# One more product by a 20-multiplication scheme, sums straight out of PSUM, and Strassen products for the two plain matrix products

## The chip, the cores and the metric

The kernel runs on one core of a Trainium2 chip. A core has a matrix engine (TensorE, PE in the profile; PEld is its loading of the stationary operand), a vector engine (VectorE, DVE), a scalar engine (ScalarE, ACT), GpSimd (POOL) and SyncE (SP), which here only issues transfers. Each works through its own instructions in order; they wait for each other by semaphores. Matrix results land in PSUM, eight banks of 512 float32 columns, here used as four pairs named b1, b3, b2_0 and b2_1. The metric is the device time of one execution in microseconds (us).

## What is computed

```python
out_lin = x @ lin_w.T + lin_b
xv = jnp.einsum('bf,efm->bem', x, weight)
zp = jnp.einsum('bf,efm->bem', jnp.square(x), jnp.square(weight))
interaction = 0.5 * jnp.sum(jnp.square(xv) - zp, axis=1)
return out_lin + interaction
```

x is 1024 x 512 (batch b, features f), weight is 64 x 512 x 512 (e, f, m), lin_w is 512 x 512, all float32. The large part is xv: a 1024 x 512 matrix times a 512 x 32768 one. Since zp is only summed over e, it needs the sum of the squared weights over e and then one 1024 x 512 by 512 x 512 product, like the linear part.

## The kernel before

The 512 columns m are taken in 22 groups: two of 16 columns, then twenty of 24 (`groups`, L133). A group has 64 times as many columns of the wide matrix, 1024 or 1536.

**Outer scheme.** Each group is one matrix product cut into 2 x 2 blocks and computed with seven block products instead of eight (Strassen in Winograd's form), taken in `ORDER` = 1, 6, 5, 2, 7, 4, 3. The operands from x, X1 to X7, are made once. The sums on the weight side (T1, T2, w12, w21) are made by transfers that add (`outer_sum`), and so are two of the sums of results (`outer_out`). The results go through the SBUF tiles oa, ob, oc and od: each product writes a `TARGET`, most add an `ADDEND` from an earlier product. A finished result is squared on ACT (`square`, L438), summed over e on DVE (`reduce`, L447) and put in `acc`. The weights' own squares and sums (`w_squares`) go to `w2_sum`.

**Inner schemes.** A block product is computed in one of two ways. `tree` (L630) is one more Strassen level: 7 products, each of two matmuls, of 384 columns in a wide group and 256 in a group of 16. `wide_tree` (L719) is a scheme for 4 x 2 blocks times 2 x 3 blocks with 20 products in place of 24, each one matmul of 256 columns; it is used for the outer products in `HK`, in wide groups only. It needs more operands of X, made by `widen` (L542) when the first wide group comes. Each matmul in float32 is two passes on PE. Both schemes start with sums of weights on POOL into tile t, keep partial sums in PSUM banks, copy some from bank to bank on ACT (L431, negated L430) so that products can go on adding to both copies, and let results leave PSUM by adds on DVE (`tt`, L413 to L421, `leave`). A tree uses b1, b3 and one of the b2 pairs; a wide tree uses one of b1 and b3 and both b2 pairs.

**How an addend comes in.** A result that leaves PSUM can have two addends: a partial sum of the same product, which is held in a tile p5 or p53 after a copy by ACT, and the outer addend. Normally DVE adds the first to the bank's content, and POOL adds the second in SBUF. For a product in `EARLY`, DVE instead adds the outer addend to a partial sum when that stands in the bank (`ahead`, or `leave` before the last product), and later adds the bank to the result, so there is neither the copy nor the add on POOL.

**Order.** The program is written as a list of operations with estimated costs (`Plan.add`). `Plan.order` plays them through like a queue on each engine, takes for PE the one with the smallest key among those that are ready, for the others the one whose latest time comes first, and so fixes each engine's order of instructions in advance. `AHEAD_OF` is a table of shifts, one for each operation, that moves latest times; SP's operations stand for the issue of transfers.

**Ends.** At the start x and lin_w are loaded, and the linear part runs as plain matmuls of 512 columns (L503): 8 row blocks x 4 parts of f. It is stored in DRAM with the bias. At the end -0.5 x squared is made on DVE (L916), `acc` and the linear part are read back and added (L930), and 32 matmuls of 512 columns (L950) multiply the squares with `w2_sum`; DVE adds both and the result is stored.

Of the kernel before, what the change touches and what calls it, by code (L numbers as in the profile page):

```python
# [12 lines left out]
AF = mybir.ActivationFunctionType  # L13
# [6 lines left out]
HK = (1, 5, 7)  # L20
EARLY = (2,)
# [14 lines left out]
SPARE = -99.0  # L36
AHEAD_OF = """
0:l 1:hvhc 2:3bp 3:hvw0 4:37v 5:338 6:3g7 7:34e 8:1o 9:33e a:33f b:-d c:369 d:-2 e:28 f:1 g:-1v h:-k i:-2k
j:-o k:-5 l:-26 m:8 n:7 o:i p:2a q:d r:15 s:b t:29 u:q v:-5 w:4 x:-k z:m 10:-9 11:d 12:-5 13:g 14:w 15:-2
16:10 17:-b 18:-e 19:17 1a:f 1b:1b 1c:l 1d:-14 1e:-c 1f:-3 1g:-11 1h:m 1i:7 1j:2 1k:8 1l:6 1m:-g 1n:-2 1o:-r  # L40
1p:-h 1q:m 1r:-r 1s:a 1t:5 1u:j 1v:-f 1w:3 1x:a 1y:o 1z:-g 20:3 21:-p 22:-g 23:g 24:2tw 25:2xs 26:f 28:38f
29:314 2a:-8 2b:-26 2c:9 2d:-4 2e:-8 2f:i 2g:-l 2h:-2 2i:d 2j:z 2k:-a 2l:13 2m:l 2n:m 2o:-7d 2p:-7 2q:-1 2r:1h
2s:-h 2t:-u 2u:ao 2v:-d 2w:-c 2x:-k 2y:7 2z:d 30:13 31:s 32:1u 33:-m 34:-j 35:-14 36:-i 37:-c 38:4 39:c 3a:18
3b:b 3c:-5 3d:l 3e:8 3f:1 3g:23u 3h:k 3i:1m 3j:g 3k:d 3l:1w1 3m:f 3n:-18 3o:-c 3p:5 3q:-i 3r:-g 3s:o 3t:-2
3u:-17 3v:3 3w:-q 3x:-t 3y:m 3z:m 40:-4 41:1rk 42:-a 43:-f 44:2 45:5 46:-1b 47:-1r 48:-4j 49:-s 4a:-t 4b:-3
4c:-o 4d:1d 4e:b 4f:2 4g:-r 4h:j 4i:-i 4j:1s 4k:-4 4l:4 4m:f 4n:3 4o:-7 4p:-l 4q:1j 4r:-b 4s:a 4t:c 4u:-2 4v:2
4w:m 4x:-1a 4y:-1 4z:-5 50:2 51:-2 52:-5 53:-5 54:r 55:x 56:13 57:n 58:20 59:1vi 5a:f 5b:-2 5c:1q 5d:-d 5e:1u1
5f:8 5g:-f 5h:3 5i:-2 5j:7 5k:36 5l:17 5m:-h 5n:-7 5o:10 5p:15 5q:i 5r:-w 5s:g 5t:f 5u:c 5v:-s 5w:1 5x:j 5y:6
5z:4d 60:e 61:13 62:d 63:-p 64:k 65:-b 66:17 67:-g 68:-k 69:-m 6a:1g 6b:x 6c:a 6d:-5 6e:5 6f:-7 6g:1e 6h:-4
6i:z 6j:-h 6k:-3h 6l:-22 6m:n 6n:-1n 6o:r 6p:y 6q:a 6r:10 6t:m 6u:-9 6v:-2 6w:2n 6x:-18 6y:-1h 6z:1 70:m  # L50
71:-1e 72:-k 73:-4 74:-3 75:-d 76:9 78:-o 79:-3 7a:-t 7b:-k 7c:-7 7d:-s 7e:b 7f:-9 7g:-1i 7h:-13 7i:19 7j:j
7k:1h 7l:-24 7m:c 7n:-2 7o:5 7p:-3 7q:q 7r:r 7s:q 7t:b 7u:1a 7v:v 7w:q 7x:-4 7y:-1p 7z:10 80:19 81:-o 82:m
83:c 84:-u 85:1 86:-1 87:-2 88:-4 89:-4 8a:-5 8b:-11 8c:3 8d:c 8e:-r 8f:x 8g:-w 8h:-u 8i:-5 8j:-1p 8k:-3
8l:-1e 8m:y 8n:o 8o:1f 8p:-1 8q:5 8r:-2 8s:1xv 8t:j 8u:7 8v:-7 8w:-f 8x:-u 8y:f 8z:1 90:e 91:6 92:-h 93:18
94:r 95:n 97:-1a 98:-c 99:-p 9a:-e 9b:8 9d:-11 9e:-3 9f:e 9g:-n 9h:-a 9j:-16 9k:-f 9l:-2 9m:h 9n:3 9o:f 9p:-5
9q:-2b 9r:v 9s:-18 9t:o 9u:o 9v:232 9w:8 9x:c 9y:-n 9z:d a0:-7 a1:-a a2:5 a3:-h a4:u a5:i a6:-d2 a7:8 a8:-n
a9:8 aa:-do ab:1a ac:i ad:-12 ae:11 af:2 ag:s ah:-n ai:-9 aj:-9 ak:3 al:l am:-fj an:-5 ao:2sx ap:d aq:13 ar:-4
as:2 at:t au:-9 av:-y aw:-l ax:-2 ay:9 az:v b0:-3 b1:-8 b2:l b3:-13 b4:g b5:-b b6:-1g b7:7 b8:-15 b9:-1 ba:-f
bc:-o bd:-b be:j bf:e bg:s bh:-1i bi:-1q bj:-1g bk:n bl:g bm:4 bn:a bo:-g bp:g bq:1 br:8 bs:-c bt:-1r bu:1e
bv:-1p bw:z bx:d by:m bz:-1f c0:-p c1:-5 c2:2 c3:q c4:-1j c5:-8 c6:j c7:e c8:-f c9:-b ca:5 cb:f cc:-k cd:1c  # L60
ce:-1n cf:-3 cg:-5 ch:-s ci:-m cj:-9 ck:-k cl:-7 cm:r cn:-a co:a cp:-n cq:-q cr:-10 cs:-w ct:b cu:-a cv:-10
cw:1g cx:-12 cy:j cz:-v d0:-14 d1:1b d2:-g d3:-g d4:8 d5:8 d6:-16 d7:n d8:j d9:-r da:-4 db:-13 dc:1d dd:-15
de:-9 df:16 dg:19 dh:d di:a dj:z dk:-a dl:-9 dm:-1w dn:-w do:-4 dp:p dq:b dr:-1w ds:2x dt:-b du:-e dv:-4 dw:3
dx:-t dy:g dz:8 e0:d e1:-5 e2:-g e3:-u e4:w e5:-r e6:j e7:4 e8:o e9:e ea:9 eb:a ec:-f ed:-16 ee:-l ef:k eg:-d
eh:-1g ei:i ej:-4 ek:-o el:-u em:5 en:-1f eo:-4 ep:5 er:7 es:s et:-1p eu:-9 ev:-b ew:o ex:i ey:-j ez:c f0:-14
f1:-u f2:-11 f3:5 f4:-l f5:c f6:-q f7:5 f8:k f9:-1 fa:-1e fb:1 fc:-1f fe:-j ff:-1 fg:5 fh:t fi:-q fj:-g fk:-8
fl:4 fm:-1o fn:10 fo:b fp:-3 fq:-13 fr:r fs:2 ft:-19 fu:1b fv:-t fw:-5 fx:-14 fy:-5 fz:-k g0:-6 g1:-6 g2:-2
g3:-1w g4:1o g6:-e g7:a g8:q g9:-d ga:-5 gb:8 gc:-h gd:9 ge:-5 gf:-7 gg:a gh:6 gi:-h gj:2 gk:-11 gl:-6 gm:4
gn:e go:1v gp:-14 gq:s gr:6 gs:-v gt:3 gu:3 gv:d gw:-6 gx:1q gy:-2 gz:-19 h0:-1m h1:-1h h2:-h h3:-5 h4:-g
h5:-14 h6:-2 h7:z h8:-j h9:f ha:-b hb:-6 hc:10 hd:-14 he:9 hf:e hg:-6 hh:-n hi:-a hj:y hk:-2 hl:-8 hn:6 ho:-t  # L70
hp:-g hq:-2 hr:-14 hs:c ht:4 hu:1 hv:a hw:-15 hx:-l hy:i hz:-d i0:-8 i1:-8 i2:-8 i3:11 i4:-7 i5:-13 i6:1h i7:b
i8:2 i9:7 ia:-8 ib:a ic:6 id:-m ie:2 if:4 ig:6 ih:-o ii:-a ij:-8 ik:n il:c im:u in:x io:-6 ip:a iq:-g ir:s
is:g it:l iu:-m iv:-1l iw:-2 ix:16 iy:-1o iz:-q j0:-y j1:-a j2:u j3:q j4:z j5:-1t j6:3 j8:-h j9:-c ja:12
# [947 lines left out]
```

## Time and profile before

| | |
|---|---|
| median of 3 runs | 1416.3 us (1412.21 to 1417.54) |
| profiled execution, own time | 1415.96 us |
| its span, first to last instruction | 1414.2 us |
| TensorE clock granted, mean | 0.997 |
| DMA | 251.76 MB, mean 178 GB/s |

The profile shows one execution. Lines name engine, source line (L464 is the matmul of the products), operation, written tile <- read tiles and form, the number of instructions after an x, then busy time and the mean of one in ns, then the idle time of the engine before them and what ended it. In the table by stretches each engine has its busy us and number of instructions, and the last three columns are the granted clock, the busy share of the transfer engines and GB/s. In the chain each row has start, length and what was worked on or waited for.

### The profile page before, as it was taken

The page shows a single profiled execution, that of the slowest core. Times are in us where ns is not written, and L with a number is a line of the kernel's source. Part 1 is how long each engine was busy: PE and PEld are TensorE (multiplying, and loading weights), DVE is VectorE, ACT ScalarE, POOL GpSimd, SP SyncE. Part 2 cuts the span into 40 slices and gives each one's busy share as a digit, 9 for nine tenths or more (in the row PEclk, how much of TensorE's full clock was granted, in tenths as well). Part 3 has the DMA queues.
Part 4 walks back from the last instruction along what each step waited for, and adds up shares of the span by engine and source line. Part 5 has one row for each costly group of instructions (what it writes and reads, how often), then busy time and mean ns, then how long its engine had stood idle before and what let it go on. Part 6 is the DMA issues. An engine that isn't in the chain of part 4 may idle for free.

```text
span 1414.2 us, 16647 instructions
## 1 busy us (share of the span) xinstructions
PE 1396.6 (99%) x5160; PEld 971.5 (69%) x5160; DVE 1100.0 (78%) x1461; ACT 806.0 (57%) x1293; POOL 1173.7 (83%) x1117
## 2 busy tenths in 40 slices
PE   8999989999999999999999999999999999999998
PEld 3887757767776766767676676777677677767663
DVE  2678678878878786887879688787968878796895
ACT  1456465656757465665656566565746556574642
POOL 5999978897979798797979879897987989788870
PEclk9999999999999999999999999999999999999999
DMA  8589596777949676795968678596958859694773
GB/s 260 164 192 227 135 202 153 165 188 161 228 120 228 160 178 171 167 223 117 230 159 192 160 180 208 131 222 146 216 143 195 197 132 221 135 238 109 163 193 112
DMA packets 92599, 251.76 MB, mean 178 GB/s; under 512 B 29472, under 2 KB 30496, under 8 KB 92512
## 3 DMA queue, kind: packets, MB, share of 16 engines
q0 software_dynamic: 26448, 134.49, 49.6%
q1 hardware_dynamic: 65488, 115.17, 24.0%
q8 instruction: 42, 0.69, 0.2%
q10 hardware_dynamic: 576, 1.05, 0.2%
q14 instruction: 45, 0.37, 0.1%
HBM read 127.04 MB, written 6.19 MB: 94 GB/s over the span
## 4 chain that ended last, share of the span: by engine, by line
PE 90%; POOL 4%; DMA 4%; DVE 1%; issue 1%; ACT 0%; SPq 0%; POOLq 0%; DVEq 0%; ACTq 0%
PE b L464 51%; PE b_r L464 18%; PE b_l L464 17%; POOL t L421 2%; PE b_r L950 1%; PE b_l L950 1%; DMA oc<-od 1%; DMA T<-T1a 1%; DMA oa<-xT 1%; PE b_l L503 1%; PE b_r L503 1%; DMA w<-weight 1%; POOL X L421 1%; DMA X<-xT 0%; POOL ob L456 0%
## 5 line engine op out<-in xcount | busy, mean ns | idle before, releaser
L464 PE MATMUL b<-t,X 128*128 128x384 f32 (+1 forms) x1504 | 518.5, 474 | 1.9 <-DVE ob L421 1.1
L464 PEld LDWEIGHTS b<-t,X 128*128 128x128 f32 x1504 | 276.1, 190 | 168.4 <-DVE oa L421 18.8
L421 POOL TENSOR_TENSOR t<-t,w 128x256 f32<-128x256 f32 (+1 forms) x200 | 232.6, 1287 | 9.0 <-PE b L464 5.7
L421 POOL TENSOR_TENSOR t<-w 128x768 f32<-128x768 f32 (+1 forms) x88 | 163.0, 1860 | 88.1 <-PE b_l L464 70.5
L438 ACT ACTIVATE oa<-oa 128x768 f32<-128x768 f32 (+1 forms) x176 | 142.8, 822 | 134.5 <-DVE oa L421 132.4
L464 PE MATMUL b<-w,X 128*128 128x384 f32 (+1 forms) x576 | 193.9, 469 | 0.1
L464 PE MATMUL b_l<-t,X 128*128 128x256 f32 x720 | 189.6, 381 | 3.9 <-ACT b_l L431 3.9
L464 PE MATMUL b_r<-t,X 128*128 128x256 f32 x600 | 167.9, 383 | 0.4 <-DVE ob L421 0.3
L447 DVE TENSOR_REDUCE acc<-oa 128x12 f32<-128x768 f32 (+1 forms) x176 | 161.6, 920 | 3.7 <-ACT oa L438 3.7
L447 DVE TENSOR_REDUCE w_sum<-wsq 128x12 f32<-128x768 f32 (+1 forms) x176 | 161.5, 920 | 1.1 <-ACT wsq L438 1.0
L464 PEld LDWEIGHTS b_l<-t,X 128*128 128x128 f32 x720 | 137.2, 191 | 32.2 <-ACT b_l L431 4.5
L464 PEld LDWEIGHTS b<-w,X 128*128 128x128 f32 x576 | 109.1, 190 | 56.5 <-ACT p L431 2.1
L464 PEld LDWEIGHTS b_r<-t,X 128*128 128x128 f32 x600 | 113.9, 191 | 47.7 <-issue 5.0
L438 ACT ACTIVATE wsq<-w 128x768 f32<-128x768 f32 (+1 forms) x132 | 107.3, 821 | 38.8 <-DVE w_sum L447 16.9
L421 DVE TENSOR_TENSOR oa<-b,oa 128x768 f32<-128x768 f32 (+1 forms) x88 | 82.0, 932 | 59.6 <-PE b L464 55.7
L421 POOL TENSOR_TENSOR t<-w,t 128x384 f32<-128x384 f32 (+1 forms) x96 | 107.7, 1122 | 2.4
L431 ACT COPY b<-b 128x768 f32<-128x768 f32 (+1 forms) x94 | 71.2, 757 | 60.3 <-PE b L464 58.0
L464 PE MATMUL b_r<-w,X 128*128 128x256 f32 x400 | 99.8, 380 | 0.0
L464 PE MATMUL b<-T,X 128*128 128x384 f32 (+1 forms) x264 | 91.3, 477 | 0.6 <-DMA T<-T1a 0.6
L421 DVE TENSOR_TENSOR oa<-b,oc 128x768 f32<-128x768 f32 (+1 forms) x66 | 61.2, 930 | 34.7 <-PE b L464 32.9
L464 PEld LDWEIGHTS b_r<-w,X 128*128 128x128 f32 x400 | 76.3, 191 | 14.3
L421 POOL TENSOR_TENSOR oc<-ob,p 128x512 f32<-128x512 f32 (+1 forms) x80 | 82.3, 1105 | 3.6 <-ACT p L431 2.0
(143 smaller groups left out, 2618.1 us busy)
## 6 DMA issues: line engine op xcount, KB each, us to landing
w<-weight SPq DMA_DIRECT2D x120, 384.0 KB, 6.0
ob<-od POOLq DMA_DIRECT2D x40, 768.0 KB, 7.9
oc<-od POOLq DMA_DIRECT2D x40, 768.0 KB, 9.5
T<-weight SPq DMA_DIRECT2D x40, 384.0 KB, 4.0
w<-T POOLq DMA_DIRECT2D x20, 768.0 KB, 6.5
T1a<-weight SPq DMA_DIRECT2D x20, 384.0 KB, 3.3
w22a<-weight SPq DMA_DIRECT2D x20, 384.0 KB, 8.8
T1a<-weight POOLq DMA_DIRECT2D x10, 768.0 KB, 11.9
```

What stands on the lines that cost most here:

```text
L421: return f(o.ap, a.ap, b.ap)
L431: return nc.scalar.copy(o.ap, i.ap)
L438: lambda _: nc.scalar.activation(o.ap, i.ap, AF.Square), i.atoms, o.atoms)
L447: nc.vector.tensor_reduce(o, x, axis=AX.X, op=ALU.add)
L464: nc.tensor.matmul(a.ap, b.ap, w.ap, start=start, stop=True, skip_group_check=True)
L503: nc.tensor.matmul(o[j].ap, x.ap[:, ts((g * 2 + j) % (NB // 2), P)], w.ap, start=(k == 0), stop=(k == NK - 1),)
L950: nc.tensor.matmul(z.ap, view(xe[h, k // KH])[:, k % KH, ts((g * 2 + j) % (NB // 2), P)], reg("w2_sum", k * M, M).ap, start=(k == 0), stop ...
```

## The change

Four parts go together.

1. Outer product 2 joins `HK`, so it goes through `wide_tree` in the twenty wide groups; X2 gets the wide operands too.
2. Products 4, 6 and 7 join `EARLY`.
3. The linear part and the product with the squares are each computed by one level of Strassen's scheme: seven products of 512 x 256 by 256 x 256, eight matmuls of 256 columns each, with sums of x and of the weights beforehand and adds afterwards. The loads at the start are cut and ordered for this, four matmuls on zeros stand at the head of PE's queue, x squared is made on ACT with a factor, and the results are added and stored by quadrants.
4. The cost estimates of copies, squares and transfers in the plan are changed, transfers of SP are put in the modelled transfer queue, and `AHEAD_OF` is a new table (90 lines before, 106 after, not shown).

```diff
-HK = (1, 5, 7)
-EARLY = (2,)
+HK = (1, 5, 2, 7)
+EARLY = (2, 4, 6, 7)
+HALF = 0.5 ** 0.5
+WARM = 4
...
-        plan.add({ACT: 0.19 + 0.00083 * o.size}, emit, i.atoms, o.atoms,
+        plan.add({ACT: 0.06 + 0.00083 * o.size}, emit, i.atoms, o.atoms,
...
-        plan.add({SP: cost}, lambda _: queue.dma_start(o, i), reads, writes, land=land)
+        plan.add({SP: 0.4}, lambda _: queue.dma_start(o, i), reads, writes, land=land, queue=moves)
...
-        plan.add({POOL: 1.0}, emit, reads + writes, writes, land=2.0, queue=3.1 * rows / 1024)
+        plan.add({POOL: 0.7}, emit, reads + writes, writes, land=1.8, queue=2.5 * rows / 1024)
...
+    lw_in(0, 0, nc.scalar)
+    x_load(0, 0, nc.sync, 2)
+    lw_in(1, 0, nc.scalar)
+    x_load(0, 1, nc.sync)
+    lw_in(0, 1, nc.scalar)
+    lw_in(1, 1, nc.scalar)
+    x_load(1, 1, nc.sync)
+    x_load(1, 0, nc.sync)
...
+    zero = reg("t", 0, P + N)
+    plan.add({DVE: 0.8}, lambda _: nc.vector.memset(zero.ap, 0.0), (), zero.atoms)
+    for n in range(WARM):
+        z, o = reg("t", 0, P), bank(f"b2_{n // 2}", n % 2)
+        zw = reg("t", P, N)
+        plan.add({PE: 1.8 * mm_cost(N)},
+                 lambda _, z=z, o=o, zw=zw: nc.tensor.matmul(o.ap, z.ap, zw.ap, start=True, stop=True),
+                 zero.atoms, o.atoms, key=-2000 + n, banks=o.banks(True))
...
+    tt(two(lsum[1]), lw(0, 1, (M, KH)), lw(0, 0, (M, KH)), only=DVE)
+    tt(two(lsum[2]), lw(1, 1, (M, KH)), two(lsum[1]), only=DVE)
+    tt(two(lsum[4]), lw(1, 0, (M, KH)), two(lsum[2]), only=DVE)
+    tt(two(lsum[7]), lw(0, 1, (M, KH)), lw(1, 1, (M, KH)), only=DVE)
...
-    tt(x_block(5), x_in(1, 1), x_in(1, 0), True)
+    tt(x_block(5), x_in(1, 1), x_in(1, 0), True, DVE)
...
-    tt(x_block(7), x_in(0, 0), x_in(1, 0), True)
+    tt(x_block(7), x_in(0, 0), x_in(1, 0), True, DVE)
...
+    def outer_products(xs, ws, base_key, ready, leave):
+
+        u2, u3, m4, m5 = "b2_0", "b1", "b3", "b2_1"
+        big("b1", xs[1], ws[1], True, base_key)
+        copy(pair(u2), pair("b1"))
+        big("b1", xs[2], ws[2], False, base_key + 1)
+        leave(0, 0, "b1")
+        big(m4, xs[4], ws[4], True, base_key + 2)
+        ready(0, m4)
+        big(m5, xs[5], ws[5], True, base_key + 3)
+        ready(1, m5)
+        big(u2, xs[6], ws[6], False, base_key + 4)
+        copy(pair(u3), pair(u2))
+        big(u3, xs[7], ws[7], False, base_key + 5)
+        leave(1, 0, u3)
+        leave(1, 1, u3)
+        big(u2, xs[3], ws[3], False, base_key + 6, ((0, 0, 2), (1, 0, 2), (0, 2, 4), (1, 2, 4)))
+        leave(0, 1, u2)
...
+    outer_products(xs, ws, 1e6, ready, leave)
```

`big` issues one such product: for each of the two parts of f, four matmuls of 256 columns, one for each block of 128 rows, into a pair of banks. In the closing stage the same function is called with the squares: its x sums are two on POOL and two on DVE, the sums of `w2_sum` are four on POOL, and the last product leaves in two halves of 512 columns, each stored by itself.

More of the change, by code (lines that the diff above doesn't have):

```diff
@@ L512, with lw, lw_in @@
[L512 to L517 removed]
+    def lw(q, c, *outer):
+        return reg("ob", KH * H + q * KH * M + c * C, C, *outer)
+    def lw_in(q, c, queue):
+        for r in range(KH):
+            o = reg("ob", KH * H + (q * KH + r) * M + c * C, C)
+            dma(o.ap, lw_src[:, q * KH + r, ts(c, C)], (), o.atoms, 0.6, 2.0, queue)
@@ new lines @@
+    other = last + 1
+    rooms = []
+    for name in (w(other, "w22"), w(other, "T1"), "w11", "X1", "X6", w(last, "T1"), "X5", "X2",
+                 "w12", "X7", "T2", "w21", "X4"):
+        rooms += [reg(name, k * 2 * N, 2 * N) for k in range(buf[name].size // (2 * N))]
+    spare = [w(other, "w22"), w(other, "T1"), "w11", w(last, "T1")]
+    spare = iter([reg(n, 2 * N, N) for n in spare])
+    rooms = iter(rooms)
+    x2 = {(h, q): next(rooms) for h, q in ((0, 0), (0, 1), (1, 1), (1, 0))}
```

405 lines of the change are left out of this document (229 added, 176 removed).

## Prediction

> **What bounds the kernel now.** I read the page first: its span, the engines' shares, the chain of work that ended last.
>
> ```profile
> span 1414.2 us, 16647 instructions
> PE 1396.6 (99%) x5160; PEld 971.5 (69%) x5160; DVE 1100.0 (78%) x1461; ACT 806.0 (57%) x1293; POOL 1173.7 (83%) x1117
> ...
> PE 90%; POOL 4%; DMA 4%; DVE 1%; issue 1%; ACT 0%; SPq 0%; POOLq 0%; DVEq 0%; ACTq 0%
> ```
>
> TensorE (PE) sets the time: 99% busy, and 90% of the chain. A mean can hide a stage, so next the table by stretches, 62.4 us each in the steady part (about one group of 24 columns), its mean over eight of them, and three other stretches:
>
> ```profile
> 312.00:374.40 62.40, 62.40 (x234) 43.62 (x233) 52.12 (x69) 38.77 (x63) 51.85 (x49) 1.00 0.80 188
> ...
> sum 499.20, PE 498.94 PEld 348.48 DVE 401.74 ACT 300.21 POOL 424.42; mean PE 62.37 PEld 43.56 DVE 50.22 ACT 37.53 POOL 53.05
> ```
> ```profile
> 36.00:187.00 151.00, 149.19 (x625) 116.55 (x624) 110.65 (x166) 81.88 (x141) 144.03 (x165) 1.00 0.76 182
> ...
> 192.00:198.20 6.20, 5.48 (x13) 4.40 (x14) 2.56 (x4) 4.13 (x8) 4.08 (x5) 0.52 0.98 192
> 1310.40:1372.80 62.40, 60.50 (x226) 42.04 (x225) 55.81 (x69) 33.74 (x56) 51.81 (x46) 1.00 0.72 171
> ```
>
> In the steady part PE has no gap, with DVE at 50.2 and POOL at 53.1 of 62.4 us. Between 36 and 187 us POOL is busy 144 of 151 us. At 192 to 198 us the clock is 0.52. From 1310 us DVE does 55.8 of 62.4 us, and there PE loses 1.9 us: remember that one. PE's own waits, two largest:
>
> ```profile
> PE b_l L503 <- DMA oa<-xT: 5.5, 1, 5.5
> PE b_l L464 <- ACT b_l L431: 3.9, 1, 3.9
> ```
>
> The chain in order of time (start, us, what) gives the pace and shows what leads to the second wait:
>
> ```profile
> 17.01 0.86 PE b_l L503 x2
> ...
> 35.89 10.49 PE b L464 x48
> ...
> 178.65 2.71 POOL t L421 x2
> 181.37 9.86 DMA w<-weight
> ...
> 192.09 0.59 ACT b_l L431
> ...
> 195.65 2.53 PE b_r L464 x6
> ...
> 239.76 15.51 PE b L464 x48
> ...
> 296.06 1.73 PE b_l L464 x8
> ...
> 1406.64 3.45 PE b_r L950 x8
> ```
>
> Each float32 product is two PE passes. A pass of 512 columns takes 0.86/2 = 0.430 us, of 384 columns 15.51/48 = 0.3231, of 256 columns 1.73/8 = 0.2163. After the wait at 192 us, at half clock, one of 256 takes 2.53/6 = 0.42. That wait hangs on POOL sums, which released a weight buffer late, then on the load, then on ACT: its queue stood on a square of those weights, with the copy that PE wanted behind it.
>
> Now the sum of the profiled run. By the code the 20 wide groups have 112 passes of 384 and 120 of 256 each; the two groups of 16 have 392 of 256; linear part and squares have 64 of 512 each: 2240 + 2792 + 128 = 5160, the page's count. Their time: 2240 x 0.3231 + 2792 x 0.2163 + 128 x 0.430 = 723.7 + 603.9 + 55.0 = 1382.6 us. Before them 5.5 us, after them 1414.2 - 1410.1 = 4.1 us (last add and store). So 1414.2 - 1382.6 - 9.6 = 22.0 us are lost inside. Of these, from the timeline's first passes:
>
> ```profile
> 5.50 2.05 PE L503 MATMUL b_l<-ob,oa 128*128 128x512 f32 x2 [5.50 <-DMA oa<-xT]
> ...
> 10.52 1.02 PE L503 MATMUL b_r<-ob,oa 128*128 128x512 f32 x2
> ```
>
> Six passes in 5.02 us instead of 2.58: 2.4 us lost to a slow clock at the start. The wait at 192 us is 3.9, and the 12 slow passes from 192.7 to 198.2 cost 5.5 - 2.6 = 2.9. The other 12.8 us are spread out. The run itself took 1415.96 us, 1.8 above its span and 0.3 below the median of the three runs (1416.3), so the sum against it is good for the median too.
>
> **The change on PE.** Product 2 in 20 groups: 28 passes of 384 (9.05 us) become 40 of 256 (8.65), a gain of 0.395 per group, 7.9 in all. Linear part and squares, each: 64 passes of 512 (27.5) become 7 products x 8 matmuls x 2 = 112 of 256 (24.2), 3.3 each. Together 14.5 us: 1368.1.
>
> **Start.** Before the data arrives, four matmuls on zeros (8 passes of 512) run. They wait for a memset of 640 columns on DVE, which I put at 0.9 us by the 768-column row below, so they start near 1.2 us. Six at 0.84 and two at 0.43 end at 1.2 + 5.0 + 0.9 = 7.1. The data came at 5.5 us before, so real work starts at 7.1, now at full clock, where before it was as far at 10.52 as a full-speed start at 7.9 would be: 0.8 us gained, not 2.4. Bounds: a gain of 2.4 if the clock rises by 5.5 us; a loss of 2.4 if passes on zeros don't raise it (rival below). The Trainium skill ("TensorE: Matmul & The Clock Gate", Part 1, The HAM clock gate) says that the array runs at half rate until about one 3.4 us window of sustained work is over; our 5.0 us at half rate is longer. By its figure four passes would be slow, the warming would end near 6.3, and the estimate would be 0.8 us lower than mine; I keep the measured 5.0.
>
> **Copies that PE waits for.** In the new scheme products 2 and 6 go on in a sum that must first be copied from one bank pair to another, 1024 columns on ACT. The nearest row is a 1024-column ACT copy, 1.04 us (below); with the hops 1.3. Each of the two stages has two such places. Products 4 and 5 don't need the copy and can fill one, and group 0's or the last group's products can fill others: 0 to 5.2 us; I take two unfilled, 2.6, since in the linear part product 4 needs a chain of three DVE sums of late-loaded weights and won't be ready at the first.
>
> **The other engines, per wide group.** Rows by form, first DVE, then POOL, then ACT:
>
> ```profile
> L447 DVE TENSOR_REDUCE acc<-oa 128x12 f32<-128x768 f32 x160 | 151.0, 944 | 3.7 <-ACT oa L438 3.7
> ...
> L421 DVE TENSOR_TENSOR oa<-oa,b 128x768 f32<-128x768 f32 x60 | 57.1, 952 | 17.0 <-PE b L464 16.2
> ...
> L421 DVE TENSOR_TENSOR oc<-ob,b_r 128x256 f32<-128x256 f32 x40 | 16.8, 419 | 5.1 <-ACT p L431 5.1
> ...
> L421 DVE TENSOR_TENSOR oc<-ob,b_l 128x512 f32<-128x512 f32 x20 | 13.6, 679 | 1.8 <-PE b_l L464 1.7
> ```
> ```profile
> L421 POOL TENSOR_TENSOR t<-w 128x768 f32<-128x768 f32 x80 | 152.1, 1908 | 88.0 <-PE b_l L464 70.5 <-DMA w<-T 10.2 <-issue 4.7
> L421 POOL TENSOR_TENSOR t<-t,w 128x512 f32<-128x512 f32 x80 | 126.2, 1578 | 8.2 <-PE b L464 5.7
> L421 POOL TENSOR_TENSOR t<-t,w 128x256 f32<-128x256 f32 x120 | 106.4, 1094 | 0.8
> ...
> L421 POOL TENSOR_TENSOR oc<-ob,p 128x512 f32<-128x512 f32 x40 | 56.1, 1410 | 0.8
> ...
> L421 POOL TENSOR_TENSOR oa<-oa,oc 128x768 f32<-128x768 f32 x20 | 47.5, 2375 | 0.1
> L421 POOL TENSOR_TENSOR t<-T,t 128x384 f32<-128x384 f32 x40 | 46.5, 1161 | 1.5
> ...
> L421 POOL TENSOR_TENSOR X<-X 128x256 f32<-128x256 f32 x43 | 37.0, 884 | 13.6 <-ACT X L431 8.4 <-DVE X L527 4.6
> L421 POOL TENSOR_TENSOR ob<-ob,oa 128x768 f32<-128x768 f32 x20 | 36.6, 1828 | 4.5 <-ACT b_l L431 4.5
> ...
> L421 POOL TENSOR_TENSOR oc<-ob,p 128x256 f32<-128x256 f32 x40 | 32.0, 801 | 2.8 <-ACT p L431 2.0
> ...
> L421 POOL TENSOR_TENSOR X<-X 128x128 f32<-128x128 f32 x21 | 12.6, 701 | 0.0
> ...
> L421 POOL TENSOR_TENSOR X<-oa 128x1024 f32<-128x1024 f32 x1 | 2.4, 2356 | 0.0
> ...
> L421 POOL TENSOR_TENSOR oc<-oc,ob 128x512 f32<-128x512 f32 x2 | 3.1, 1540 | 0.0
> ```
> ```profile
> L431 ACT COPY p<-b 128x768 f32<-128x768 f32 x60 | 47.5, 792 | 24.1 <-PE b L464 24.0
> ...
> L431 ACT COPY b_r<-b_l 128x512 f32<-128x512 f32 x60 | 34.9, 582 | 6.8 <-PE b_l L464 6.8
> ...
> L431 ACT COPY X<-oa 128x1024 f32<-128x1024 f32 x2 | 2.1, 1044 | 1.6 <-DMA oa<-xT 1.6
> ```
>
> DVE: product 2 has six 768 adds now (5.71) and gets five of 512 and ten of 256 (3.40 + 4.19 = 7.59): +1.9. Product 7 gets its first addend straight from PSUM: two more of 512, three of 256, and one 512 split in two 256: +2.8. Products 4 and 6 get one more 768 each: +1.9. In all +6.6, so 56.8 us of about 61.6. POOL: product 2's operand sums grow from 1.91 + 2 x 1.16 = 4.2 to 1.91 + 2 x 1.58 + 4 x 1.09 = 9.4; away go product 7's adds (2 x 1.41 + 3 x 0.80 = 5.2) and those of 6 and 4 (1.83 + 2.38): -4.2, so 48.9. ACT: four more copies of 512 (2.3) and a small one against one of 768 (0.8) in product 2; two 768 copies and two smaller ones less elsewhere: about -0.6. So the near-full helper changes from POOL to DVE, at 92% of PE's group. DVE's work has two kinds: the weight and result reductions (24 x 0.94 = 22.7 us a group) can come late, while the adds must free PSUM banks in time. I price the tightness at 0.2 us a group, 4 us in all: from below 0 (the steady groups now show no wait), from above 1.9 us a group, what PE lost at 1310 us with DVE at 89%. Nearer to zero, because the loss at 1310 us came while the closing stage's work was squeezed in.
>
> **POOL-bound stretch, 36 to 187 us.** Two sums of X go from POOL to DVE (-2 x 2.36), widening X2 adds 5 x 0.88 + 7 x 0.70 = 9.3, the two groups of 16 lose six adds of 1.54 (-9.2), group 2 has -4.2: about -9 us of 144. PE arrives about 4 us earlier, POOL about 9, so the wait at 192 us shrinks or moves if it hangs on POOL. The load and its place in ACT's queue come from the new order, which no view of before shows. I take half of 3.9 + 2.9 away: -3.4, bounds -6.8 and +4.
>
> **Closing stage.** x squared goes from DVE to ACT, two adds of X to POOL and two to DVE: DVE ends lighter. The last add of 512 columns and its store stay as they are: 4.1 us.
>
> **Sum.** 7.1 + 1368.1 + 4.1 = 1379.3; lost time 22.0 - 2.4 (start, counted in the 7.1) + 2.6 + 4.0 - 3.4 = 22.8; span 1402.1, and 1.8 around it: 1403.9, rounded to 1404.
>
> **Rivals.** *DVE becomes the bound* (slower). Its idle time falls from 12.2 us a group to 61.6 - 56.8 = 4.8; as it executes in order, it waits whenever the head of its queue stands on PE. If it needs more than 4.8 us a group of such waits, PE waits for banks. Three products with 20 small products each now follow one another (5, 2, 7), and each holds three of the four bank pairs, so fewer other products are there to fill in. At the 1.9 us of the stretch at 1310 us: 38 instead of 4, 1438. For: that row. Against: POOL was busy 95% from 36 to 187 us, and PE was still busy 149.2 of 151. *The head takes the gain back*: if loads, not POOL, hold the end of the first 190 us, the 3.3 + 0.8 us of the linear part and the 3.4 become waiting there, 1404 + 7.5 = 1411. A new wait of over 3 us would cost more than its length: the one of 3.9 us cost 2.9 besides, one of the linear part would do the same. The Trainium skill (same page, HAM oscillation) has a rule for this, that gaps above about 3.4 us put the clock back to half; the trace agrees at 3.9 us. *The head becomes clean*: all 6.8 us gone and no tightness: 1404 - 3.4 - 4 = 1397. *Zeros don't warm*: the eight passes last 8 x 0.84 = 6.7 to 7.9 us, and the next 5 us are slow too: 0.8 + 2.4 = 3.2 more, 1407.
>
> **How the numbers follow.** The measurement tells 0.5%, 7.1 us, from no change: faster is below 1409.2, slower above 1423.4. Chances: my forecast 0.47, clean head 0.17, zeros 0.08, head takes back 0.14 (0.03 of it still below 1409.2), DVE bound 0.14 (0.01 of it mild, within 0.5%). Faster 0.75, same 0.12, slower 0.13. The range runs from 1393 (clean head, with the copies filled and the clock up early) to 1416; it leaves out the DVE case and the low tail.
>
> **What would show it.** Steady groups: PE period 61.6 us with DVE near 56 and POOL near 49 busy; waits of PE on DVE adds of some tenths a group at most. Start: eight passes on zeros from about 1.2 us, the first six at 0.84 us, real passes at 0.216 us from about 7 us. The linear part's end before 33 us (35.9 now). Wrong it is if PE's waits on DVE or ACT are over 0.5 us a group, if DVE has hardly any idle time, or if a wait of over 3 us with a slow clock stands in the first 200 us again.

## The result and the profile after

The change made the kernel slower: 1438.2 us (median; 1437.59 to 1440.22) against 1416.3, ratio 1.0162, 95% interval 1.0139 to 1.0185. Forecast were 1404 and a range up to 1416. The profiled execution took 1437.59 us, its span 1435.8. First the page: span, engines, chain.

```profile
span 1435.8 us, 17687 instructions
...
PE 1409.5 (98%) x5504; PEld 1024.8 (71%) x5504; DVE 1224.1 (85%) x1809; ACT 792.7 (55%) x1296; POOL 1088.4 (76%) x1067
...
PE 80%; POOL 6%; DMA 6%; DVE 3%; ACT 3%; issue 2%; SPq 0%; ACTq 0%; POOLq 0%; DVEq 0%
```

PE is still at 98%, but 10% of the chain has moved from it to the others. The table by stretches, of the length of one group each, has helpers as forecast and a period that is not:

```profile
600.16:663.43 63.27, 63.05 (x244) 45.23 (x244) 57.24 (x86) 37.96 (x63) 49.06 (x50) 1.00 0.73 177
663.43:726.70 63.27, 63.00 (x245) 45.54 (x245) 53.77 (x82) 35.28 (x59) 48.05 (x44) 1.00 0.72 177
...
sum 253.08, PE 252.10 PEld 181.60 DVE 222.14 ACT 146.86 POOL 194.34; mean PE 63.03 PEld 45.40 DVE 55.54 ACT 36.72 POOL 48.59
```

With the prediction's own pass times a group's work on PE is 84 x 0.3231 + 160 x 0.2163 = 61.7 us, before the change 112 x 0.3231 + 120 x 0.2163 = 62.1. The period was 62.4 and is 63.3. So 0.3 us a group were lost before and 1.5 are now, and yet "PE busy" shows 63.0 of 63.3: the losses are pieces of 0.08 to 0.4 us, many of them no idle time at all in the table, since a pass counts as busy until its modelled end.

They show when one takes, from the first pass on data, the start of each pass minus the start of the one before, and subtracts the time that the earlier one needs by itself (0.2155 us for 256 columns, 0.3225 for 384, as in stretches without a wait). Differences above 0.03 us, summed from the trace, in us:

| stretch (us of the span) | before | after | in a new order (r_after_y, below) |
|---|---|---|---|
| 0 to 62 | 3.5 | 5.0 | 5.8 |
| 62 to 248 | 11.1 | 11.2 | 6.0 |
| 248 to 1302 | 5.5 | 28.7 | 5.6 |
| 1302 to the end | 3.0 | 12.9 | 5.2 |
| all | 23.2 | 57.9 | 22.6 |

So the steady groups lost 23 us more, the end 10 more, and the first 248 us 1.6 more: the wait at 192 us is gone, and as much came back ahead of it.

**One place of the steady part.** The timeline of product 2's first sums (start, length, engine, what; in brackets the idle time before and what ended it):

```profile
602.23 0.68 DVE L437 TENSOR_TENSOR oa<-oa,b_l 128x512 f32<-128x512 f32 x1
...
602.94 0.57 ACT L447 COPY b_r<-b_l 128x512 f32<-128x512 f32 x1 [0.23 <-DVE oa L437]
...
603.54 0.69 DVE L437 TENSOR_TENSOR oa<-oa,b_l 128x512 f32<-128x512 f32 x1 [0.64 <-ACT b_r L447]
603.60 0.37 ACT L447 COPY p<-b_r 128x256 f32<-128x256 f32 x1
...
604.14 0.74 DVE L437 TENSOR_TENSOR oa<-oa,b_r 128x256 f32<-128x256 f32 x2
...
605.03 0.67 PE L480 MATMUL b_r<-w,X 128*128 128x256 f32 x2 [0.17 <-DVE oa L437]
```

Three readers want the bank T (b_l): two early additions on VectorE and one copy on ScalarE. No one writes it, yet they stand one behind the other: addition, copy (0.03 us after it), addition (0.03 us after the copy), with VectorE idle for 0.64 us. On bank U (b_r) the copy (603.60) also stands ahead of the additions (604.14), but these show no wait of their own: VectorE came to them only then, late from T. The pass that needs U comes 0.17 us late, and the two passes take 0.67 us together where two of 0.38 us, 0.2155 apart, take 0.59: another 0.08. So in this program reads of one bank by two engines wait for each other, as a read and a write do. The Trainium skill ("PSUM — Partial Sum Buffer", PSUM bank collisions raise a hardware error) gives a reason: two engines on one bank at once raise an error and read wrong data, reads against reads included. The order in the trace agrees; that it would fail otherwise no run here shows. Neither the plan nor the prediction had this rule. The largest waits of VectorE from 250 to 1310 us (total us, times, longest) that come of it:

```profile
DVE oa L437 <- ACT b_r L447: 11.1, 17, 0.7
...
DVE oc L437 <- ACT b_r L447: 6.5, 9, 0.7
```

Waits of this kind are not new, though. The kernel before has them at other copies, for example

```profile
DVE od L421 <- ACT od L430: 6.7, 17, 0.4
DVE od L421 <- ACT od L431: 5.8, 17, 0.4
```

Counting every wait of 0.15 us and more of ScalarE and VectorE for each other that goes back to nothing but a bank that both read, VectorE waits 31 us and ScalarE 21 in the kernel before, 35 and 13 in the changed one. New is the place: the copies and additions of products 2 and 7 now stand right ahead of a bank that PE wants, where in the kernel before all losses of the steady part were 5.5 us.

**Handovers without reserve.** Matching each product of 256 columns with the last work of another engine that it needs gives a simple rule: if that work ends 0.15 us or more before PE is free, nothing is lost (0.04 us at most); at 0 to 0.15 us the product is 0.03 to 0.18 us late, 0.10 in the mean; later than that the wait itself comes on top (32 products with a release 0.1 to 0.2 us after PE was free lost 0.35 us each). Of 1331 such products in the steady part 135 were below 0.15 us, of 1020 in the kernel before 9. The 135 lost 27 of the 28.7 us, and none of the steady part's waits of PE is for a transfer.

These losses stand at a few places that come back from group to group. In product 5, 17 times, the last release is a ScalarE copy that first waited 0.49 us for a VectorE read of the same bank; PE loses 5.8 us there:

```profile
599.72 0.38 ACT L446 ACTIVATE od<-b_r 128x256 f32<-128x256 f32 x1 [0.49 <-DVE od L437]
```

The place on bank U above, 17 times, costs 5.2 us. Behind 59 ScalarE copies of 512 columns from bank to bank PE loses 8.8 us; in 15 of them a wait for a shared read stands earlier in ScalarE's queue, and 37 had waited for nothing but PE's own pass. The changed plan hands such banks over at the edge: it gives such a copy a slot of 0.485 us (0.615 before), and the trace has 0.57 us and more from start to end.

**The end.** Timelines of VectorE, of GpSimd and of PE:

```profile
1384.95 0.95 DVE L437 TENSOR_TENSOR oa<-b,oc 128x768 f32<-128x768 f32 x1
1385.82 4.93 DVE L1051 SCALAR_TENSOR_TENSOR X<-w,X 128x1024 f32<-128x1024 f32 x1
1390.68 1.81 DVE L437 TENSOR_TENSOR oa<-b,oc 128x768 f32<-128x768 f32 x2
```
```profile
1385.56 1.74 POOL L472 DMA_DIRECT2D ob<-od  x2
1386.71 2.96 POOL L437 TENSOR_TENSOR X<-w22a,X 128x1024 f32<-128x1024 f32 x1
```
```profile
1391.68 2.92 PE L480 MATMUL b<-t,X 128*128 128x384 f32 x4 [3.39 <-DVE oa L437]
```

One addition of the closing stage in SBUF takes 4.93 us, beside an addition of GpSimd in SBUF, and PE waits 3.39 us behind it; its next four passes take 2.92 us, at half clock (granted 0.50), where four such passes take 1.45 at 616.87 us. The Trainium skill ("SBUF — State Buffer", SBUF: two separate sides) says that an operation of VectorE with two SBUF inputs and one of GpSimd lock a shared pair of ports, so that one stands until the other is done; the trace agrees in so far as the addition, though it began 0.9 us before GpSimd's by the profile, ends 1.1 us after it, about its own length (1.22 us where it runs alone, x7 below).

### The profile page after: what moved, and what is told of

Its sections match the earlier page's. It is cut to its first block, busy times and chain, and to the rows that moved or that the text cites. A ratio compares the mean times of both kernels' runs of the same rounds, so it can differ in the third digit from the quotient of the medians.

```text
span 1435.8 us, 17687 instructions
## 1 busy us (share of the span) xinstructions
PE 1409.5 (98%) x5504; PEld 1024.8 (71%) x5504; DVE 1224.1 (85%) x1809; ACT 792.7 (55%) x1296; POOL 1088.4 (76%) x1067
## 4 chain that ended last, share of the span: by engine, by line
PE 80%; POOL 6%; DMA 6%; DVE 3%; ACT 3%; issue 2%; SPq 0%; ACTq 0%; POOLq 0%; DVEq 0%
PE b L480 36%; PE b_r L480 22%; PE b_l L480 20%; POOL t L437 3%; PE b L537 2%; DVE oa L437 2%; POOL X L437 1%; DMA oc<-od 1%; DMA ob<-od 1%; DMA w<-T 1%; DMA ob<-lin_wT 1%; ACT b_l L447 1%; DVE w_sum L463 1%; DMA T<-weight 1%; ACT od L446 1%
## 5 line engine op out<-in xcount | busy, mean ns | idle before, releaser
L480 PE MATMUL b<-t,X 128*128 128x384 f32 (+1 forms) x1184 | 400.7, 471 | 5.9 <-DVE oa L437 3.4
L437 POOL TENSOR_TENSOR t<-t,w 128x512 f32<-128x512 f32 (+1 forms) x300 | 294.9, 991 | 113.2 <-PE b L480 86.8
L480 PE MATMUL b_l<-t,X 128*128 128x256 f32 x960 | 247.6, 381 | 0.4 <-ACT b_l L447 0.3
L480 PE MATMUL b_r<-t,X 128*128 128x256 f32 x800 | 225.6, 386 | 3.7 <-ACT b_l L447 1.1
L480 PE MATMUL b_l<-w,X 128*128 128x256 f32 x480 | 121.1, 385 | 1.3 <-ACT b_l L447 1.2
L447 ACT COPY b<-b 128x768 f32<-128x768 f32 (+2 forms) x78 | 59.8, 767 | 95.3 <-PE b L480 53.2
L480 PE MATMUL b<-w,X 128*128 128x384 f32 (+1 forms) x336 | 107.6, 456 | 1.3 <-DMA w<-T 1.3
L480 PEld LDWEIGHTS b_l<-w,X 128*128 128x128 f32 x480 | 88.6, 190 | 21.9 <-ACT b_l L447 9.6
L437 DVE TENSOR_TENSOR ob<-b,oa 128x768 f32<-128x768 f32 (+1 forms) x88 | 80.4, 930 | 15.2 <-PE b L480 7.4
L454 ACT ACTIVATE oc<-oc 128x768 f32<-128x768 f32 (+1 forms) x88 | 69.9, 819 | 37.1 <-DMA oc<-od 37.1
```

Of the source, the lines that this page charges most:

```text
L437: return f(o.ap, a.ap, b.ap)
L447: return nc.scalar.copy(o.ap, i.ap)
L454: lambda _: nc.scalar.activation(o.ap, i.ap, AF.Square), i.atoms, o.atoms)
L480: nc.tensor.matmul(a.ap, b.ap, w.ap, start=start, stop=True, skip_group_check=True)
```

## The experiments

The forecast's own rival was the **load theory** (VectorE, 55.5 of 63.3 us, is the bound). Against it stood the **bank theory** (shared reads), and a **table or order theory** (a fixed order planned on times that the chip does not have). Losses below are counted as in the table.

**Shared reads taken away, copies' side** (x1_copies_sbuf). The values of these copies are left out.

```diff
-        copy(h("S"), h("T"))
+        copy(h("S"), h("T"), source=reg(f"X{i}", 0, 2 * V) if early else None)
...
-        copy(p19, h("U", 1))
+        copy(p19, h("U", 1), source=reg(f"X{i}", 0, V) if early else None)
```

> The changed kernel in its own order, but in products 2 and 7 ScalarE's two copies out of banks T and U (S<-T of 512 columns, p19<-U of 256) take their input from a constant SBUF tile instead, so they read no bank that VectorE reads (their values are left out). Bank theory (the program makes ScalarE's and VectorE's reads of one bank wait for each other, and with the early sums of products 2 and 7 that holds up the release of T and U): the group goes from 63.3 us to 62.0 to 62.5, so the median to 1412 to 1423. Load theory (VectorE's 55.5 us of 63.3 is the bound): VectorE's work is unchanged, so 1432 to 1439. Table theory (the written-out order is fitted to durations that the chip doesn't have): the stalls move elsewhere, over 1430.

Measured 1430.5 us (1428.6 to 1432.3), ratio to before 1.0102 (1.0083 to 1.0122): 7.7 less than the changed kernel, between the theories. The waits of VectorE on these copies are gone, steady losses fall from 28.7 to 21.8, and PE's wait in the row below goes (PE's passes of one form between 263 and 1300 us: number, busy us, mean ns, idle before them), first the changed kernel, then this one; 379 ns is what the form took in the kernel before:

```profile
L480 PE MATMUL b_r<-w,X 128*128 128x256 f32 x487 | 123.3, 384 | 1.5 <-DVE oa L437 1.2
```
```profile
L482 PE MATMUL b_r<-w,X 128*128 128x256 f32 x492 | 122.4, 379 | 0.0
```

So taking the pairs on T and U away gives 7 to 8 us, a third of the steady loss. The place that I expected to pay for all of it paid for a part. The edit also frees these two copies from waiting for PE's passes into T and U, and 3.3 us were lost anew behind sums of GpSimd, so the figure is not exactly the price of the shared reads.

**The additions' side** (x4_adds_sbuf): `tt(f(o, *at), f(a, *at), h(b, half), sub)` reads a constant SBUF tile instead of T and U.

> The other half of the same pairs is taken away: ScalarE copies T and U as before, and VectorE's four early additions on T and U in products 2 and 7 read a constant SBUF tile instead of the bank (their values are left out); VectorE has as many instructions and columns as in the changed kernel. Bank theory: the same gain as with the copies taken away, 1412 to 1423, since either partner alone holds nobody up. Load theory: 1432 to 1439. Table theory: over 1430.

Measured 1481.8 us (1480.0 to 1487.2), 1.0471 (1.0445 to 1.0496). A failed experiment: with both inputs in SBUF an addition of 512 columns takes 1.27 us, where it took 0.68 out of PSUM, and one of 256 takes 1.21 for 0.41 (rows by form):

```profile
L437 DVE TENSOR_TENSOR oa<-oa,X 128x512 f32<-128x512 f32 x40 | 49.9, 1266 | 0.0
L437 DVE TENSOR_TENSOR oa<-oa,X 128x256 f32<-128x256 f32 x40 | 47.0, 1212 | 0.0
```

So it changed VectorE's times as well and tells nothing of banks. What it shows is the price of an SBUF addition beside GpSimd's sums, as at the end of the changed kernel.

**VectorE's load taken down** (x2_short_wsq): `reduce` of the weights' squares over 4 of 64 columns, the others left out of the sums.

> The changed kernel in its own order, with the eight sums of squares of the weights per group cut from 12x64 to 12x4 columns (the other columns are left out of the sums): by 0.944 us for 768 columns and about 0.08 fixed, each falls to some 0.13, so VectorE loses 8 x 0.81 = 6.5 us a group and stands at 49, as in the kernel before (50.2). Load theory: the group falls back to 62.0 to 62.5, median 1412 to 1423. Bank theory: the pairs on T and U stay, so most of the loss stays: 1430 or more. Table theory: over 1430.

**VectorE's load put up in the kernel before** (x3_before_twice_wsq): the same eight reductions emitted twice.

> The kernel before, in its own order, with each of the eight sums of squares of the weights per group made twice: 8 x 0.944 = 7.5 us more on VectorE, 57.7 of 62.4 us a group, more than the changed kernel's 55.5. Nothing else is changed, and no further bank is read by two engines. Load theory: it loses as the change did, 1 us a group or more, so 1436 or more. Bank theory: under 0.4 us a group, so under 1425. Table theory: some 1425 to 1436, as the longer slots fall out of the planned order.

x2: 1441.2 us (1439.0 to 1443.2), 1.0180 (1.0157 to 1.0203), not faster than the change (1.0162), with VectorE down by 120 us:

```profile
PE 1411.2 (98%) x5504; PEld 1025.8 (71%) x5504; DVE 1103.9 (77%) x1809; ACT 790.6 (55%) x1296; POOL 1087.5 (76%) x1067
```

x3: 1507.1 us (1504.2 to 1512.9), 1.0649 (1.0620 to 1.0677), far above all expectations; its chain:

```profile
PE 65%; DVE 27%; issue 4%; ACT 2%; DMA 1%; POOL 1%; DVEq 0%; SPq 0%; ACTq 0%
```

In x2 120 us less on VectorE give nothing: in this order load is not what binds. In x3 148 us more (1247.7 busy after 1100.0) cost 91. My reading, which no run isolates, is that each extra reduction stands ahead of an addition that was planned for just that moment; 27% of the chain is now on VectorE. The load theory falls as an account of the change; that VectorE has room to spare falls with it.

**All shared reads taken away** (x5_all_copies_sbuf): besides x1's two, the copies out of S and V in products 5 and 1.

```diff
-            copy(n5, h("S", 1))
+            copy(n5, h("S", 1), source=reg(f"X{i}", 0, V))
...
-                copy(d, x, sub)
+                copy(d, x, sub, source=reg(f"X{i}", 0, x.n) if b in "SV" else None)
```

> As with the copies of T and U taken away, and besides ScalarE's copies out of bank S and bank V in products 5 and 1 (n5, and the cells that are written straight from S and V) read a constant SBUF tile, so that no bank of a wide product is read by both engines at its end (these values are left out too). Bank theory: in the run without the copies of T and U one stall of 0.34 us a group was left, ended by ScalarE's copy out of S ahead of product 5's last pass (17 of them, 5.8 us with the pass behind each); it goes, so 1430.5 - 5.8, 1421 to 1427. Theory that it is only the tightness of a long order: the stall moves to the next place and the time stays at 1428 to 1433.

Measured 1436.3 us (1432.7 to 1439.2), 1.0134 (1.0104 to 1.0164). The stall ahead of product 5's last pass did go, and the steady losses fell on, from 21.8 to 18.5; but PE lost 4.66 us behind a VectorE sum into ob at 1339 us, and 2.37 us at 1360, where the changed kernel loses less, so the whole run is only 1.9 us faster than the changed kernel and misses its expectation. In sum: shared reads are about 10 of the 23 us, which fits the 5.8 and 5.2 us read from the changed kernel's trace; the rest is elsewhere, and the table theory's "it moves on" holds for the end.

**The end** (x7_sum_later): one instruction in another place.

```diff
+    ordered = plan.order()
+    at = {op.n: k for k, (op, _) in enumerate(ordered)}
+    moved = ordered[at[6601]]
+    ordered.insert(at[6537] + 1, moved)
+    ordered.remove(moved)
```

> The changed kernel, all its work, with one instruction of the end stage in another place of VectorE's order: the addition of the stored linear part and the summed products (1024 columns, it took 4.93 us at 1385.82 while GpSimd added a block of the squares) stands behind the last five sums of product 4 instead of ahead of four of them. End theory (of the 10 us that the end lost, this one instruction costs its wait of 3.56 us, the half clock behind it, some 1.3 us, and little more): 1438.2 - 5, 1432 to 1435. If the whole of VectorE is late by then, the next sums wait as long and the time stays at 1436 to 1439.

Measured 1435.9 us (1434.5 to 1436.5), 1.0149 (1.0130 to 1.0168): 2.4 less, half of what was expected. In its profile the addition takes 1.22 us instead of 4.93, PE's wait and the half clock are gone, and from the pass that waits for ob (at 1348.5 us, in the changed kernel at 1345.3) to the end it is 85.7 us instead of 90.5:

```profile
1393.33 1.22 DVE L1051 SCALAR_TENSOR_TENSOR X<-w,X 128x1024 f32<-128x1024 f32 x1
```

So this place costs 2.4 to 4.8 us.

**Reserve of the handovers** (x8_before_late_copies): the kernel before, each ScalarE copy out of a wide product's bank behind one of 64 columns.

```diff
+            if i.alone:
+                return [nc.scalar.copy(late[:, :], Reg(i.tile, i.off, 64, alone=True).ap), full()]
```

> The kernel before, all its work and its own order, with ScalarE's copies out of banks in products 1, 5 and 7 each given a copy of 64 columns of the same bank into a spare tile ahead of it: about 0.11 us later each, as much as the changed planner's ScalarE costs (0.06 + 0.00083 a column where it had 0.19) take from each copy's reserve. VectorE's work and the reads shared by the two engines stay as they are. Reserve theory (a pass whose bank is released less than 0.15 us before PE wants it costs 0.1 us and more, and the changed plan hands over at that edge): passes that had 0.2 to 0.3 us of reserve fall under the edge, 4 to 12 us more, 1420 to 1428. Bank theory alone: the reads of S and V that follow one another get later too, but that is two places a group; under 3 us, 1415 to 1419. Load theory: ScalarE's load of 38 of 62 us binds nothing, 1415 to 1419.

Measured 1418.0 us (1416.6 to 1419.7), 1.0021 (1.0010 to 1.0033): 3 us, less than the reserve theory wanted, more than nothing. The kernel before had most releases 0.3 us and more ahead of PE, so 0.11 us brings few to the edge. This run does not settle the size.

**New orders for the whole work.** The rest are kernels that leave nothing out. Their planner has further rules, and the table of shifts was searched again under them. The first (r_after_a, and r_before_a for the kernel before) knew only the rule on shared reads and 0.09 us for a pass after a wait:

```diff
         def ready(o):
-            return max([0.0] + [d.end for d in o.waits]) + self.HOP
+            t = max([0.0] + [d.end for d in o.waits])
+            for other in {ACT, DVE} - set(o.costs):
+                if len({ACT, DVE} & set(o.costs)):
+                    t = max([t] + [read_end.get((at, other), 0.0) for at, w, _ in o.banks if not w])
+            return t + self.HOP
```

> The changed kernel's work without any cut, in an order made anew: in the planner a read of a bank by ScalarE now waits for VectorE's last read of that bank and the other way round, a pass that starts after a wait costs 0.09 us more, and the table of head starts was searched again under these rules. Every engine has the work of the changed kernel (VectorE 55 us a group). Bank and order theory: the group comes down from 63.3 us to 61.6 to 62.0, as the forecast had it, and the kernel to 1400 to 1412. Load theory: VectorE has as much to do as before the new order, so 1425 or more.

> The kernel before, all its work, in an order made anew under the same two rules, as the counterpart of the changed kernel's new order. Its waits cost some 0.5 us a group (9.0 us in 17 groups), so a better order can give at most that: 1405 to 1417. If it gains as much as the changed kernel's new order does, then the search is what helps, and not the rule on banks.

1453.9 us (1451.8 to 1455.5), 1.0255 (1.0224 to 1.0285), and 1436.6 (1430.1 to 1449.9), 1.0149 (1.0089 to 1.0209): both worse than the orders they came from. In the changed kernel's, PE lost 19 us of steady time behind sums into ob that waited for a transfer sum (VectorE waited 37.5 us for these, below), and 8.5 behind those into w21; the planner had most kinds of these transfers landing 1.6 to 3.4 us earlier than they do here (medians, counted from the issue). So a search fits the order to whatever the planner has wrong.

```profile
DVE ob L447 <- DMA ob<-od: 37.5, 17, 3.4
```

The next had handovers and transfers as the traces show them: a bank goes to PE 0.25 us after ScalarE's slot (0.18 before), adding transfers land 1.5 us (r_after_w) or 2.5 us (r_after_v) later, the closing additions keep clear of GpSimd. r_after_nc is r_after_w with the rule on shared reads taken out, searched as long; r_before_u is the kernel before.

> The changed kernel's work without any cut, ordered anew by a planner that knows what the traces show: reads of one bank by ScalarE and VectorE follow one another, a bank goes over to PE 0.25 us after ScalarE's slot and 0.235 after VectorE's (durations of 0.57 us for a slot of 0.48, plus the 0.15 us that PE needs to load weights unseen), adding transfers land 1.5 us later than the changed planner has it, and the added sums of the end stage keep clear of GpSimd's. Theory that the loss is the order's (pairs on banks, handovers without reserve, a few transfers): the group falls to 61.6 to 62.0 and the time to 1400 to 1412. Load theory: VectorE has the same 55 us a group, so 1430 or more.

> As the other new order of the changed kernel, but with the adding transfers planned 2.5 us later, so with more room ahead of what waits for them. Order theory: 1402 to 1414; if the first new order's misses (stalls behind adding transfers) were the reason for its 1454 us, this one has none over 1 us in the steady groups. Load theory: 1430 or more.

> As the new order with 1.5 us for the transfers, searched as long, with one rule left out: this planner lets ScalarE and VectorE read one bank at the same time. On the chip they still follow one another. Bank theory: it loses what the pairs cost, 7 us or more against the order with the rule, so some 1410 to 1425. If the pairs cost nothing by themselves, it lies within 3 us of the order with the rule.

> The kernel before, all its work, ordered anew by the same planner with all the rules (transfers 0.5 us later, since its own estimates were right in the middle). Its losses in the steady groups are 0.3 us a group, so there is little to gain: 1403 to 1418. It shows what the new planner does for a kernel with one product less in the wide scheme: if the new order of the changed kernel is faster than this, the change has its gain, and only the table hid it.

| run | us (range) | ratio to before (95%) |
|---|---|---|
| r_after_w | 1433.9 (1432.5 to 1436.8) | 1.0148 (1.0131 to 1.0164) |
| r_after_v | 1430.0 (1425.9 to 1433.8) | 1.0117 (1.0089 to 1.0144) |
| r_after_nc | 1444.3 (1443.6 to 1445.4) | 1.0220 (1.0204 to 1.0235) |
| r_before_u | 1454.0 (1448.5 to 1461.1) | 1.0274 (1.0250 to 1.0299) |

All four missed the numbers of the theory that they were made for, and those of r_after_w and r_after_v are what the load theory had said (1430 or more); that this is chance shows further down, where the same load runs at 1402. Only the comparison of r_after_nc with r_after_w came out as the bank theory had it: 10.4 us for one rule in the planner (two orders from two searches, so part of it may be luck; further down two such lie 7.5 us apart). The waits of VectorE's early sums on ScalarE's copies speak for the rule, r_after_nc, then r_after_w:

```profile
DVE oc L467 <- ACT b_r L477: 10.9, 16, 0.7
DVE oa L467 <- ACT b_r L477: 10.8, 16, 0.7
```
```profile
DVE oa L468 <- ACT b_r L478: 8.4, 8, 1.0
```

What was left in r_after_v stood in two places: product 6's copy on ScalarE behind a square that waited for the transfer sum into oc (17.4 us of steady losses) and sums of GpSimd (7.9). ScalarE's timeline at one of them:

```profile
391.20 0.84 ACT L485 ACTIVATE oc<-oc 128x768 f32<-128x768 f32 x1 [1.83 <-DMA oc<-od]
391.95 0.79 ACT L478 COPY b<-b 128x768 f32<-128x768 f32 x1
```

So the last planner has the landing of each kind of transfer later, by 0.6 to 4.9 us, as read from that trace:

```diff
+LATE = {
+    POOL: {'ob': 3.4, 'oc': 4.9, 'T2': 4.4, 'w12': 4.4, 'T1a': 0.9, 'T1b': 0.9, 'w21': 0.6},
+    SP: {'w21': 3.5, 'w22a': 4.0, 'w22b': 4.0, 'w11': 2.5, 'T2': 2.7, 'w12': 1.2},
+}
...
+            if o.queue:
+                o.land += LATE[next(iter(o.costs))].get(o.tile, 0.5)
```

> The changed kernel's work without any cut, ordered by the planner with the rule on shared reads and real handovers, and now with the landing of each kind of transfer as the last order's trace had it (4.9 us after the old estimate for the sums into oc, 4.4 for those into T2 and w12, 3.4 for ob), the loads of the head in the changed kernel's order, and the table searched from the changed kernel's own. In the order with 2.5 us for all, two places cost 25 us together: ScalarE's copy in product 6 behind a square that waited for the sum into oc (17.4 us) and GpSimd's sums (7.9). Order theory: these go, the group comes to 62.0 or less, 1403 to 1416, at or below the kernel before. If the transfers move again and a new place waits, 1420 to 1432. Load theory: 1430 or more.

> A second order found under the same rules by another search (it started from the order with 2.5 us for all transfers; the planner likes it less). Order theory: the same signs, a few us above the first, 1408 to 1425. It shows how far two orders that the planner holds to be near each other lie apart on the chip.

r_after_y: **1402.2 us** (1401.7 to 1402.9), ratio to before 0.9914 (0.9896 to 0.9931), just below the order theory's 1403 to 1416. r_after_y2, a second order: 1409.7 (1407.3 to 1410.9), 0.9961 (0.9950 to 0.9972). Page and groups of r_after_y:

```profile
span 1400.3 us, 17786 instructions
...
PE 1383.1 (99%) x5504; PEld 1036.2 (74%) x5504; DVE 1224.1 (87%) x1809; ACT 787.1 (56%) x1296; POOL 1094.0 (78%) x1067
```
```profile
sum 247.88, PE 247.88 PEld 183.78 DVE 222.27 ACT 145.48 POOL 195.08; mean PE 61.97 PEld 45.94 DVE 55.57 ACT 36.37 POOL 48.77
```

VectorE does the same 1224.1 us and 55.6 a group as in the changed kernel, and PE's group is 61.97 us instead of 63.3. The waits of VectorE's early sums on ScalarE's copies into b_r are down from 17.6 us (the first two rows of waits) to 4.9, though all of VectorE's waits for shared reads only from 35 to 28: where they stand counts, not how long they are. The last column of the first table has what else went.

The control is the kernel before under the same rules (transfer landings from its own trace) and an equal search, two orders:

> The kernel before, all its work, with the same treatment as the 1402.2 us order of the changed kernel: shared reads, real handovers, transfers landing as its own trace has them, loads of the head kept, and a search as long from its own table. It tells what of the 12.7 us below the kernel before is the change and what is the planner. Its passes take 1382.6 us and 9.6 lie before and after them; with as little lost as the changed kernel's new order (some 16 to 21 us) it comes to 1408 to 1415. If it comes to 1402 or less, the change is worth nothing and the planner all; if it stays at 1412 or more, nearly all is the change.

> A second order of the kernel before from another search under the same rules, that the planner holds to be as good: 1406 to 1425. The better one of the two is what the changed kernel's better one is to be compared with.

1414.9 us (1411.3 to 1417.6), 1.0004 (0.9988 to 1.0020), and 1410.5 (1408.4 to 1411.0), 0.9978 (0.9967 to 0.9988). The planner alone is worth 3 us at best for the kernel before, and 36 for the changed one. Best order against best order the change's work is 8.3 us faster (1402.2 and 1410.5), of the 12 forecast; second against second 5.2 (1409.7 and 1414.9). Two such orders of one kernel lie 4 to 8 us apart, so neither figure is sharp.

## Why the prediction was wrong

**What held.** PE's passes: 5504 of them, 61.7 us a group (the period of 61.6 us that the prediction names is below its own passes; it is no term of the sum). The head: eight passes on zeros from 1.59 us, real work at 7.03 (forecast 7.1). That number is partly luck: the zeros began 0.4 us later than forecast, and the half rate lasted 3.9 us and not 5.0:

```profile
1.59 2.07 PE L556 MATMUL b_l<-t 128*128 128x512 f32 x2 [1.59 <-DVE t L551]
...
6.17 1.02 PE L556 MATMUL b_r<-t 128*128 128x512 f32 x2
7.03 1.46 PE L537 MATMUL b<-ob,oa 128*128 128x256 f32 x6
```

The helpers' loads: 55.5, 48.6 and 36.7 us a group against 56.8, 48.9 and 36.9. The copies that PE waits for: one in each stage, 1.3 and 1.2 us, as forecast.

**What failed is the step "I price the tightness at 0.2 us a group, 4 us in all".** It measured 1.3 us a group, 23 us from 248 to 1302. I took the missing waits in the steady groups of before for a sign that there was room. They showed that the old order kept a reserve, and the change brought a new order planned with ScalarE slots 0.13 us shorter, and with early additions that read the banks that ScalarE copies at that moment. I did price the additions on VectorE, but as load alone; who else reads a bank, and in which order they must, I did not ask. The diff showed both. The prediction's own sign, waits of PE on VectorE or ScalarE over 0.5 us a group, would not have shown it either: from 250 to 1310 us the profile names only these two, 2.2 us in all.

```profile
PE b_r L480 <- DVE oa L437: 1.2, 7, 0.2
PE b_l L480 <- ACT b_l L447: 1.0, 2, 0.7
```

**The rival that ended at 1438 had the right number for a wrong reason.** "DVE becomes the bound" took 1.9 us a group from a stretch with VectorE at 89%. VectorE's load did not bind: x2 took 5.7 us a group away and gained nothing, and r_after_y runs at 61.97 us with the same load. Shared reads account for some 7.7 us (x1) to 11 (the two places read from the trace; steady losses of x5 and r_after_nc against r_after_w give 10). The other 12 to 15 us are handovers and waits that a better planned order also removes; r_after_y shows that they belong to the order. Their largest part in the trace, 8.8 us, stands behind ScalarE's copies of 512 columns, 44 of these 59 without a shared read ahead, which fits slots planned short; but no run made the changed kernel's order with the old slots, so how they divide stays open.

**The end was not priced:** "DVE ends lighter" looked at sums and not at place. It lost 9.9 us more, 8.6 more than the one copy in the forecast, of which x7 gives 2.4 to 4.8 to a single addition that ran beside GpSimd's.

**The stretch to 187 us:** I took 3.4 us away and nothing went: the wait at 192 us vanished, and 62 to 186 us lost 9.5 instead of 4.2. That was the rival "the head takes the gain back", in that part.

Sum: of the 4.0 for tightness 3.4 belong to the 17 steady groups. 1402.1 + (23.2 - 3.4) steady + (1.6 + 2.4 - 1.3 + 3.4) up to 248 us, for the start, the copy and the stretch that were in the forecast, + 8.6 end - 0.6 (the rest of the 4.0) = 1436.0; the span was 1435.8. And r_after_y, with a span of 1400.3 for the same work, shows that the rest of the sum was sound.

## What to carry to other kernels

When an order is fixed in advance, price a change by its handovers and not by loads: for each bank that changes hands list all its readers on both engines, count them one after the other, and ask for 0.15 us of reserve ahead of PE. A search over an order finds every place where its planner is too kind; check the planner's slots, hops and transfer landings against a trace before believing its gain. To tell a lost idea from a lost order, take load away in the same order, then make the order anew: here the first gave nothing and the second 36 us.

## What the runs showed of the hardware

Passes on zeros raise the clock like any others: with them the half rate lasted 3.9 us here (from 1.59 to about 5.5) and 4.9 in r_after_y, without them 4.8 in the kernel before; it began with PE's first pass each time. A release 0 to 0.15 us ahead of PE costs 0.03 to 0.18 us, though by the profile's rows PE hardly waits for it. An addition on VectorE with both inputs in SBUF was 1.9 to 2.9 times as long beside GpSimd's sums as one out of PSUM of the same size, and one of 1024 columns took 4.93 us instead of 1.22. Sums by transfer landed 0.4 to 2.6 us later, counted from their issue, than the changed planner had them (medians of each kind, changed kernel's trace). Half clock also came behind waits below the 3 us that the prediction named: in r_after_a behind one of 2.45 us and one of 2.49 (at 259 and 519 us, granted clock 0.50), while one of 3.10 us at 15.5 us had none (clock 1.00).
